# Row statistics of the closing stage scaled two pairs at a time on GpSimd, with norm, sum and store one turn later

## The chip, the core and the metric

The kernel runs on one core of a Trainium2 chip. A core has a matrix engine (TensorE, "PE" in the profile, with its weight loads as "PEld"), a vector engine (VectorE, "DVE"), an activation engine (ScalarE, "ACT"), a general engine (GpSimd, "POOL") and a small engine that here only starts transfers between the on-chip memory and DRAM (SyncE, "SP"; its list of issues is "SPq" in the profile). Each engine works through its own instructions in order and waits on semaphores for the others. The metric is the device time of one execution in microseconds; less is better.

## What is computed

The reference is a block of two residual layers on `x` of shape (8, 2048, 512), float32:

```python
x = x + _layernorm(_L0_attn_ref(_layernorm(x), ...))   # a long convolution from a state space model, then GELU
x = x + _layernorm(_L0_ffn_ref(_layernorm(x), ...))    # a gated recurrence over 8 steps and a last layer

def _layernorm(x, axis=-1, eps=1e-05):
    m = jnp.mean(x, axis=axis, keepdims=True)
    v = jnp.var(x, axis=axis, keepdims=True)
    return (x - m) / jnp.sqrt(v + eps)

# the end of _L0_ffn_ref
h = jnp.tanh(jnp.einsum('tbi,oi->tbo', x, wo) + c_final @ uo.T + bo)
```

The closing stage computes the last line of each: `h = tanh(z + u)`, with `z = x wo` already in DRAM and `u = c_final uo + bo`, then the layer norm of `h` over 512 values, and `x + norm(h)`, which is the output.

## The kernel before

The 2048 positions lie as 16 chunks of 128 partitions; 8 batch rows belong to each chunk. The recurrence runs over four quarters of four chunks each. The outputs of the first three quarters are made by `head` beside the matrix products of the next quarter. The last quarter has nothing after it: its outputs are made by `tail` (L1153), when the matrix products are over. This closing stage is what the change touches.

`tail` handles a pair of rows (two batch rows of one chunk, a 128x2x512 float32 block, 512 KB). The last quarter has 16 such pairs, numbered 0 to 15 here. For one pair there are these parts:

- `load` (L1162): SP loads the pair's `z` from DRAM. Each has a place of its own in the room of former weights.
- `load_x` (L1174): SP loads the pair's residual input `x` (`x1_d`; "x_d" in the profile). Nine places serve pairs 0 to 8. Pairs 9 to 14 use the places of pairs 0 to 5 again, so each of these six loads has to wait until the output of the pair nine places earlier has been stored from there. Pair 15 has a place of its own.
- `sum_` (L1179, L1180): twice an add of `u` on VectorE and a tanh on ScalarE.
- `stat` (L1183): `lnstat` (L462 to L465) on VectorE, two bn_stats, two bn_aggr and one small add of eps to the two variances; then `lnscale` (L471 to L476) on GpSimd, a power of -0.5, a product with the mean and a sign, on 128x2 values each.
- `norm` (L1187): ScalarE applies scale and bias to the two rows.
- `out` (L1192): the residual add of the two rows, on GpSimd; in every fourth pair the second row is added on VectorE.
- `store` (L1195): SP writes the pair to the output.

The order on each engine is written out by hand: the functions are called in the order in which the engines are to run them, inside `manual_schedule`, and this includes SP's issues. The loop at L1290 goes through turns n. In each it calls the parts by the list at L1293, whose second number is the delay: part `st_` is called for pair n - d. So turn n issues the load of `z` for pair n + 3, the load of `x` for pair n + 3, the store of pair n - 5, the sum of pair n - 1, the statistics of pair n - 2, and the norm and output add of pair n - 3. The first three pairs' loads and six further loads of `z` are issued earlier, so the loop issues `z` for pairs 9 to 15 and `x` for pairs 3 to 15. Every fourth turn also adds the bias to `u` of one chunk (L1098, VectorE).

Since SP's list is in order, a load that waits for a store to land holds back everything behind it in the list.

Of the kernel before, what the change touches and what calls it, by code (L numbers as in the profile page):

```python
# [11 lines left out]
F32 = mybir.dt.float32  # L12
I32 = mybir.dt.int32
AF = mybir.ActivationFunctionType
ALU = mybir.AluOpType
# [4 lines left out]
P = 128  # L20
# [9 lines left out]
EPS = 1e-5  # L30
# [29 lines left out]
def s4_gated_block(ctx, tc, a, dbg=None):  # L60
    nc = tc.nc
    V, S, T, Q = nc.vector, nc.scalar, nc.tensor, nc.gpsimd
# [41 lines left out]
    nhalf = const.tile([P, NB], F32, name="nhalf")  # L104
# [347 lines left out]
        T.matmul(out, lhsT=w(0), rhs=x(1), start=False, stop=stop)  # L452


    def lnstat(src, tag):

        n = len(src)
        st = FE.tile([P, n, 6], F32, name="st" + tag)
        mv = FE.tile([P, n, 2], F32, name="mv" + tag, bufs=2)
        rs = FE.tile([P, n], F32, name="rs" + tag, bufs=2)  # L460
        for i, v in enumerate(src):
            V.bn_stats(st[:, i], v)  # L462
        for i in range(n):
            V.bn_aggr(mv[:, i], st[:, i])
        V.tensor_scalar(rs, mv[:, :, 1], EPS, None, ALU.add)  # L465
        return n, mv, rs, tag

    def lnscale(s_, neg=True):

        n, mv, rs, tag = s_  # L470
        Q.tensor_tensor(rs, rs, nhalf[:, 0:n], ALU.pow)  # L471
        mu = mv[:, :, 0]
        if neg:
            mu = FE.tile([P, n], F32, name="nm" + tag, bufs=2)
            Q.tensor_tensor(mu, mv[:, :, 0], rs, ALU.mult)
            Q.tensor_scalar(mu, mu, -1.0, None, ALU.mult)  # L476
        return [(mu[:, i : i + 1], rs[:, i : i + 1]) for i in range(n)]
# [101 lines left out]
    with ExitStack() as cctx:  # L579
# [182 lines left out]
        for k in range(4):  # L762
            pmt = pm_.tile([P, 512], F32, name="pmt")
            lv, src = ((0, None), (0, 0), (1, 0), (1, 1))[k]
# [42 lines left out]
        for g in range(NG):  # L807
# [12 lines left out]
            if not nxt:  # L820
                ectx.close()
                FV = ctx.enter_context(tc.tile_pool(name="fv", bufs=1, side="right", reuse_waits="tile"))
                FE = ctx.enter_context(tc.tile_pool(name="fe", bufs=1, side="right", reuse_waits="tile"))
                fcol = FE.tile([P, 4, KT], F32, name="fcol")
            with tc.manual_schedule(engines=MAN if nxt else MAN | {mybir.EngineType.SP}):
# [17 lines left out]
                for s_ in range(NJ):  # L843
                    if s_ % 2 == 0 and s_:
                        conv_out(g, s_ // 2 - 1)
                    if nn:

                        d = ND1 if g == 1 else 0
# [125 lines left out]
    def part_a(key):  # L974

        q, t, kind, n = key
        z = kind == "z"
        u = units[key] = pu.tile([P, 4, BP], F32, name="u")
        for pr in FIRST:
            mms(u, places(key, pr), *views(key)[0], True, not t or z)  # L980
        if t and not z:
            mms(u, FIRST[0][:1] + FIRST[1] + FIRST[0][1:], *views(key)[1], False, True)
        if z:
            if n == 0:
                gates["z"] = FT.tile([P, 2, BP], F32, name="zc")
            c22 = gates["z"][:, n]
        else:
            g = gates[key] = FJ.tile([P, 4, BP], F32, name="gate2", tag="wq") if kind == 2 else FT.tile([P, 4, BP], F32, name=f"gate{kind}")
            c22 = g[:, 2]
        z_, v_ = (UV, UZ) if z else (UZ, UV)  # L990
        u2 = u2p[:, len(u2s) % 2]
        u2s.append(key)
        S.activation(u2, u[:, UX], AF.Copy)  # L993
        V.tensor_tensor(u2, u2, u[:, UY], ALU.add)  # L994
        V.tensor_tensor(c22, u2, u[:, z_], ALU.add)
        V.tensor_tensor(c22, c22, u[:, v_], ALU.add)
        V.tensor_tensor(u[:, 2:4], u[:, 2:4], u2[:, None].to_broadcast([P, 2, BP]), ALU.add)  # L997

    def part_b(key):

        q, t, kind, n = key
        u, z = units.pop(key), kind == "z"
        wx, wc = views(key)
        mms(u, places(key, THEN), *wx, False, z or not t)
        if z:
            zt, zc = FT.tile([P, 3, BP], F32, name="zt", bufs=2), gates["z"]
            S.activation(zt[:, 0], u[:, UX], AF.Copy)
            S.activation(zt[:, 1:3], u[:, 2:4], AF.Copy)

            def store():  # L1010
                o = z_d[QC * q + n, :, t], z_d[QC * q + n + 2, :, t]
                dma(out=o[0], in_=zt[:, 0:2].rearrange("p a b -> p (a b)"))
                dma(out=o[1][:, 0:BP], in_=zt[:, 2])
                dma(out=o[1][:, BP:], in_=zc[:, n])

            return store
        if t:
            mms(u, THEN, *wc, False, True)
        g = gates[key]
        bs = (bias if t else bias0)[:, kind]  # L1020
        act = lambda o, s_, b: S.activation(o, s_, AF.Tanh, scale=gsc[kind], bias=b)  # L1021
        act(g[:, 2], g[:, 2], bs[:, n + 2 : n + 3])
        act(g[:, 0:2], u[:, 0:3:2], bs[:, n : n + 1])
        act(g[:, 3], u[:, UZ], bs[:, n + 2 : n + 3])
        if kind == 2:
            V.scalar_tensor_tensor(g, gates.pop((q, t, 1, n)), 1.0, g, ALU.add, ALU.mult)  # L1026
        elif kind == 0:
            return state(q, t, n)
# [124 lines left out]
    def tail(q, cj, tp, n):  # L1153

        c, s_ = QC * q + cj, {}

        def load():
            w = (3, 1, 5, 2, 6, 0)[n // 3]
            if n % 3 == 0:
                tails[w] = (FW if w < 2 else FV if w == 2 else FT).tile([P, 3, 2, H], F32, name="zz", tag=f"w{w}", bufs=1)  # L1160
            s_["z"] = tails[w][:, n % 3]
            dma(out=s_["z"], in_=z_d[c, :, 2 * tp : 2 * tp + 2])  # L1162

        def load_x():
            i = (n + 3) % 9
            if n == 15:
                s_["x"] = tails[0][:, 1]
            elif i < 3:
                if i == 0:
                    tails[4] = FT.tile([P, 3, 2, H], F32, name="xw", tag="w4", bufs=1)  # L1170
                s_["x"] = tails[4][:, i]
            else:
                s_["x"] = (FJ, FJ, FE, FT, FJ, FT)[i - 3].tile([P, 2, H], F32, name="xx", tag=("wl", "ws", "y", "gate1", "wq", "gate0")[i - 3])
            dma(out=s_["x"], in_=x1_d[c, :, 2 * tp : 2 * tp + 2])  # L1174

        def sum_():
            for i in range(2):
                z = s_["z"][:, i]
                V.tensor_tensor(z, z, us_[c], ALU.add)  # L1179
                S.activation(z, z, AF.Tanh, scale=1.0 / SW)  # L1180

        def stat():
            s_["s"] = lnscale(lnstat([s_["z"][:, i] for i in range(2)], "h"))  # L1183

        def norm():
            for i, (nm, rs) in enumerate(s_["s"]):
                S.activation(s_["z"][:, i], s_["z"][:, i], AF.Identity, scale=rs, bias=nm)  # L1187

        def out():
            for i in range(2):  # L1190
                z, x = s_["z"][:, i], s_["x"][:, i]
                (V if n % 4 == 3 and i else Q).tensor_tensor(x, x, z, ALU.add)  # L1192

        def store():
            dma(out=a["out"][c, :, 2 * tp : 2 * tp + 2], in_=s_["x"])  # L1195

        return load, load_x, sum_, stat, norm, out, store

    tails = {}
    gsc = (0.5 / SW, 0.5 / SW, 1.0 / SW)  # L1200
    bias = FE.tile([P, 3, KT], F32, name="bias")
    bias0 = FE.tile([P, 3, KT], F32, name="bias0")
# [11 lines left out]
    def put(fs, base, ps):  # L1214
        for f, p in zip(fs, ps):
            todo.setdefault(base + p, []).append(f)

    def go(p):
        for f in todo.pop(p, ()):
            f()  # L1220
# [12 lines left out]
    rows = [tail(NQB - 1, cj, tp, 4 * cj + tp) for cj in range(QC) for tp in range(NB // 2)]  # L1233
# [4 lines left out]
    for n, (q, t) in enumerate(steps):  # L1238
        b = 16 * n
# [15 lines left out]
        if q and t:  # L1255
            for r in range(QC * NB):
                p = 3 * r + 17 - 16 * t
                if 0 <= p < 16:
                    put(head(q - 1, r // NB, r % NB), b, [p + d for d in (0, 2, 4, 6, 8, 9, 10, 12)])
    with tc.manual_schedule(engines=MAN | {mybir.EngineType.SP}):  # L1260
        before = None
        for n, (q, t) in enumerate(steps):
            zs = [(q, t, "z", i) for i in range(2)]
            gs = [(q, t, gt, mp) for mp in range(2) for gt in (1, 2, 0)]

            def finish(key, p):
                st_ = part_b(key)
                if st_:
                    put([st_], p, [1])

            for sl, key in enumerate(zs + gs if n else gs[:5] + zs + gs[5:]):
                p = 16 * n + 2 * sl
                part_a(key)
                go(p)

                late = n and t and sl == 2
                if sl == 3 and n and t:
                    finish(zs[1], p + 1)
                    before = gs[0]
                if before and not late:  # L1280
                    finish(before, p + 1)
                if not late:
                    before = key
                go(p + 1)
        part_b(before)
        for p in sorted(todo):
            go(p)
        for f in end[2:6]:
            f()
        for n in range(len(rows) + 5):  # L1290
            if n % 4 == 0 and n < len(rows):
                end[6 + n // 4]()
            for st_, d in ((0, -3), (1, -3), (6, 5), (2, 1), (3, 2), (4, 3), (5, 3)):  # L1293
                if 0 <= n - d < len(rows) and (st_ > 1 or n - d > (2 if st_ else 8)):
                    rows[n - d][st_]()

# [61 lines left out]
```

## Time and profile before

| what | value |
|---|---|
| median of 3 runs | 2808.93 us (2808.02 to 2810.8) |
| the profiled execution, its own time | 2808.14 us |
| its span, first to last instruction | 2806.4 us |
| busy over the span: PE, DVE, ACT, POOL | 2552.5, 2095.5, 1480.0, 1226.8 us |
| last matrix product of the last quarter's steps ends | about 2724 us |
| first sum of pair 0 on VectorE | 2737.68 us |
| sum of pair 15 on VectorE starts | 2789.56 us |
| last store issued, landed | 2802.80, 2805.4 us |

Times inside the execution count from the start of the span. The profiled execution's own time is 1.74 us more than its span. The matrix engine sets the time up to about 2737 us; the closing stage is the last 69 us, some 2.4% of the whole.

### The profile page before, as it was taken

The page shows a single profiled execution, that of the slowest core. Times are in us where ns is not written, and L with a number is a line of the kernel's source. Part 1 is how long each engine was busy: PE and PEld are TensorE (multiplying, and loading weights), DVE is VectorE, ACT ScalarE, POOL GpSimd, SP SyncE. Part 2 cuts the span into 40 slices and gives each one's busy share as a digit, 9 for nine tenths or more (in the row PEclk, how much of TensorE's full clock was granted, in tenths as well). Part 3 has the DMA queues.
Part 4 walks back from the last instruction along what each step waited for, and adds up shares of the span by engine and source line. Part 5 has one row for each costly group of instructions (what it writes and reads, how often), then busy time and mean ns, then how long its engine had stood idle before and what let it go on. Part 6 is the DMA issues. An engine that isn't in the chain of part 4 may idle for free.

```text
span 2806.4 us, 60001 instructions
## 1 busy us (share of the span) xinstructions
PE 2552.5 (91%) x23940; PEld 2229.7 (79%) x23940; DVE 2095.5 (75%) x4248; ACT 1480.0 (53%) x3091; POOL 1226.8 (44%) x1520
## 2 busy tenths in 40 slices
PE   4578888896999999999999999999999999999991
PEld 3367777785888888788898887888898788888870
DVE  7878888867667766677887777778777677777748
ACT  8966666654444444445555444455555454554436
POOL 5777777743112211124554431355554224543307
PEclk9799999998999999999999999999999999999995
DMA  6977887887334433225564432356554234543356
GB/s 236 304 238 241 259 257 246 257 282 209 99 86 126 106 98 91 80 91 150 164 180 138 142 102 95 109 162 178 155 165 129 91 106 136 166 121 102 104 170 234
DMA packets 507536, 449.25 MB, mean 160 GB/s; under 512 B 275574, under 2 KB 386680, under 8 KB 502264
## 3 DMA queue, kind: packets, MB, share of 16 engines
q1 hardware_dynamic: 506824, 444.90, 52.7%
q8 instruction: 187, 3.06, 0.4%
q14 instruction: 93, 0.76, 0.1%
q10 hardware_dynamic: 432, 0.52, 0.1%
HBM read 293.58 MB, written 151.78 MB: 159 GB/s over the span
## 4 chain that ended last, share of the span: by engine, by line
PE 62%; DVE 7%; ACT 3%; issue 1%; POOL 1%; DMA 0%; SPq 0%; POOLq 0%; DVEq 0%; ACTq 0%
PE u L955 60%; PE pt L485 2%; DVE zz L1179 1%; ACT gate L1021 1%; DVE u L997 1%; DVE cd L1042 1%; DVE gate L1041 0%; DVE cf L1056 0%; DVE sth L462 0%; ACT xf L101 0%; DVE u2p L994 0%; DVE xf L102 0%; PE u L451 0%; ACT zr L1145 0%; ACT cf L1054 0%
## 5 line engine op out<-in xcount | busy, mean ns | idle before, releaser
L955 PEld LDWEIGHTS <-w 128*128 128x128 f16 x15120 | 1481.0, 98 | 198.9 <-issue 16.0
L955 PE MATMUL u<-xf,w 128*128 128x256 f16 x8064 | 944.2, 273 | 17.8 <-DVE u L997 6.1
L955 PE MATMUL u<-cf,w 128*128 128x256 f16 x7056 | 825.7, 273 | 2.0 <-DVE cf L1056 2.0
L1021 ACT ACTIVATE gate<-u,bias 128x512 f32<-128x512 f32 (+1 forms) x384 | 200.9, 574 | 275.2 <-PE u L955 274.9
L993 ACT ACTIVATE u2p<-u 128x256 f32<-128x256 f32 x256 | 96.6, 379 | 436.9 <-PE u L955 436.8
L955 PE MATMUL u<-w,xf 128*128 128x256 f16 x2688 | 310.5, 273 | 4.0 <-DVE u L997 4.0
L1146 POOL TENSOR_TENSOR x1r<-x1r,zr 128x512 f32<-128x512 f32 x96 | 133.4, 1390 | 410.5 <-ACT zr L1145 295.2
L994 DVE TENSOR_TENSOR u2p<-u2p,u 128x256 f32<-128x256 f32 x256 | 106.7, 417 | 267.3 <-ACT u2p L993 265.9
L909 POOL TENSOR_TENSOR xr<-y,xr 128x512 f32<-128x512 f32 x120 | 160.7, 1360 | 300.0 <-ACT y L908 300.0
L955 PEld LDWEIGHTS <-xf 128*128 128x128 f16 x2688 | 263.0, 98 | 36.3 <-DVE u L997 5.5
L997 DVE TENSOR_TENSOR u<-u,u2p 128x512 f32<-128x512 f32 x256 | 179.0, 699 | 8.7
L646 POOL TENSOR_TENSOR u<-xg,u 128x512 f16<-128x512 f32 x104 | 129.2, 1242 | 106.7 <-ACT u L644 105.6
L471 POOL TENSOR_TENSOR rsy<-rsy,nhalf 128x2 f32<-128x2 f32 (+1 forms) x68 | 51.0, 751 | 281.6 <-DVE rsy L465 280.6
L640 POOL TENSOR_TENSOR xg<-xg,mu 128x512 f32<-128x512 f32 x112 | 162.8, 1460 | 6.0 <-DMA xg<-in_xr 6.0
L102 DVE TENSOR_TENSOR x<-pxt,x 128x256 f16<-128x256 f32 x240 | 100.1, 419 | 63.6 <-ACT x L101 62.3
L1026 DVE SCALAR_TENSOR_TENSOR gate<-gate,gate 128x1024 f32<-128x1024 f32 x64 | 90.0, 1406 | 69.6 <-ACT gate L1021 68.5
L1128 POOL TENSOR_TENSOR zr<-zr,ur 128x512 f32<-128x512 f32 x96 | 130.0, 1354 | 21.1 <-DMA zr<-z_d 12.3
L666 PE MATMUL pxt<-x,at 128*128 128x256 f16 x224 | 61.9, 277 | 79.3 <-DVE x L102 78.9
L462 DVE BATCH_NORM_STATS2 sty<-y 128x6 f32<-128x512 f32 x120 | 76.9, 682 | 76.1 <-DMA y<-y_d 76.1
L101 ACT ACTIVATE x<-pxt 128x256 f16<-128x256 f32 x240 | 91.5, 382 | 73.5 <-PE pxt L666 67.8
L451 PE MATMUL pyt<-u,t 128*128 128x128 f16 (+2 forms) x544 | 123.7, 227 | 0.0
L452 PE MATMUL pyt<-u,t 128*128 128x128 f16 (+2 forms) x544 | 123.3, 227 | 0.0
(373 smaller groups left out, 5261.1 us busy)
## 6 DMA issues: line engine op xcount, KB each, us to landing
xs<-in_rr SPq DMA_DIRECT2D x32, 1024.0 KB, 6.4
t<-kpad SPq DMA_DIRECT2D x32, 1024.0 KB, 5.6
y_d<-y SPq DMA_DIRECT2D x30, 1024.0 KB, 7.6
xr<-in_r SPq DMA_DIRECT2D x60, 512.0 KB, 5.8
xa<-x_d SPq DMA_DIRECT2D x120, 256.0 KB, 4.0
y<-y_d SPq DMA_DIRECT2D x59, 512.0 KB, 5.8
x_d<-xr SPq DMA_DIRECT2D x59, 512.0 KB, 3.1
xg<-in_xr SPq DMA_DIRECT2D x28, 1024.0 KB, 8.6
```

The lines of the kernel that those rows point to most:

```text
L102: V.tensor_tensor(lo, src, hi, ALU.subtract)
L451: T.matmul(out, lhsT=w(1), rhs=x(0), start=False, stop=False)
L452: T.matmul(out, lhsT=w(0), rhs=x(1), start=False, stop=stop)
L640: Q.tensor_tensor(xg, xg, bc(mu1), ALU.subtract)
L646: (V if g == 2 else Q).tensor_tensor(u[:, js, 1], xg, u[:, js, 0], ALU.subtract)
L909: Q.tensor_tensor(xv, yv, xv, ALU.add)
L955: T.matmul(u[:, d], lhsT=w(f, b, i == 1, k), rhs=x(f, b, i == 2, k), start=opens and bank not in seen, stop=stop and j == len(n) - 1, skip ...
L994: V.tensor_tensor(u2, u2, u[:, UY], ALU.add)
L997: V.tensor_tensor(u[:, 2:4], u[:, 2:4], u2[:, None].to_broadcast([P, 2, BP]), ALU.add)
L1021: act = lambda o, s_, b: S.activation(o, s_, AF.Tanh, scale=gsc[kind], bias=b)
L1128: Q.tensor_tensor(s_["z"], s_["z"], us_[c], ALU.add)
L1146: Q.tensor_tensor(s_["x"], s_["x"], s_["z"], ALU.add)
```

## The change

The statistics of a pair (`stat`) no longer include the eps add and the scale. They write mean and variance into one half of a buffer that two pairs share. A new part, `scale`, does something only for odd pairs: it takes the variances of two pairs together (128x2x2 values) and runs four GpSimd instructions, the eps add, the power, the product and the sign. The list of the turns becomes

```python
for n in range(len(rows) + 6):
    ...
    for st_, d in ((0, -3), (6, 6), (1, -3), (2, 1), (3, 2), (4, 4), (5, 4), (7, 2)):
```

so norm and output add are called for pair n - 4, the store for pair n - 6, and there is one turn more. On SP, a turn's order changes from z, x, store to z, store, x.

```diff
-    def lnstat(src, tag):
+    def lnstat(src, tag, eps=True):
...
-        V.tensor_scalar(rs, mv[:, :, 1], EPS, None, ALU.add)
+        if eps:
+            V.tensor_scalar(rs, mv[:, :, 1], EPS, None, ALU.add)
...
         def stat():
-            s_["s"] = lnscale(lnstat([s_["z"][:, i] for i in range(2)], "h"))
+            m = n % 2
+            if m == 0:
+                both[0] = [FE.tile([P, 2, *d], F32, name=nm, bufs=2) for nm, d in (("mvb", (2, 2)), ("rsb", (2,)))]
+                both[0] += [FE.tile([P, 2, 2], F32, name="nmb", bufs=2)]
+            mv, rs, nm = s_["b"] = both[0]
+            st = FE.tile([P, 2, 6], F32, name="stb", bufs=2)
+            for i in range(2):
+                V.bn_stats(st[:, i], s_["z"][:, i])
+            for i in range(2):
+                V.bn_aggr(mv[:, m, i], st[:, i])
+
+        def scale():
+            if n % 2:
+                mv, rs, nm = s_["b"]
+                Q.tensor_scalar(rs, mv[:, :, :, 1], EPS, None, ALU.add)
+                Q.tensor_tensor(rs, rs, nhalf[:, 0:4].rearrange("p (a b) -> p a b", a=2), ALU.pow)
+                Q.tensor_tensor(nm, mv[:, :, :, 0], rs, ALU.mult)
+                Q.tensor_scalar(nm, nm, -1.0, None, ALU.mult)
 
         def norm():
+            mv, rs, nm = s_["b"]
+            s_["s"] = [(nm[:, n % 2, i : i + 1], rs[:, n % 2, i : i + 1]) for i in range(2)]
             for i, (nm, rs) in enumerate(s_["s"]):
...
-        return load, load_x, sum_, stat, norm, out, store
-
-    tails = {}
+        return load, load_x, sum_, stat, norm, out, store, scale
+
+    tails, both = {}, {}
...
-        for n in range(len(rows) + 5):
+        for n in range(len(rows) + 6):
...
-            for st_, d in ((0, -3), (1, -3), (6, 5), (2, 1), (3, 2), (4, 3), (5, 3)):
+            for st_, d in ((0, -3), (6, 6), (1, -3), (2, 1), (3, 2), (4, 4), (5, 4), (7, 2)):
```

The other callers of `lnstat` keep the eps add on VectorE.

## The prediction

> **What bounds the kernel now.** I read three views in this order: the stage table (busy time by engine), the order of time on VectorE and GpSimd, and SP's waits with the landing times of single transfers. The change acts only after 2737 us, where the matrix engine has nearly finished. Columns of the first: stretch, its length, then busy time of PE, PEld, DVE, ACT, POOL, TensorE clock, DMA share, GB/s.
>
> ```profile
> 2737.68:2748.46 10.78, 7.00 (x33) 2.95 (x31) 10.57 (x25) 7.59 (x12) 4.76 (x8) 1.00 0.01 6
> 2748.46:2781.58 33.12, 0.00 (x0) 0.00 (x0) 32.27 (x68) 23.63 (x37) 29.78 (x43) 0.52 0.82 268
> 2781.58:2797.00 15.42, 0.00 (x0) 0.00 (x0) 14.27 (x28) 9.65 (x15) 13.87 (x20) 0.50 0.92 339
> 2797.00:2806.40 9.40, 0.00 (x0) 0.00 (x0) 1.41 (x1) 1.52 (x2) 5.60 (x7) 0.50 0.44 175
> ```
>
> VectorE is full (32.27 of 33.12), GpSimd nearly (29.78), and the transfers are busy 0.82 of the time: three near limits, not one. VectorE's fullness is partly a wait:
>
> ```profile
> 2749.57 1.27 DVE L462 BATCH_NORM_STATS2 sth<-zz 128x6 f32<-128x512 f32 x2
> 2750.77 0.29 DVE L464 BATCH_NORM_AGGREGATE mvh<-sth 128x2 f32<-128x6 f32 x2
> 2751.17 1.15 DVE L465 TENSOR_SCALAR rsh<-mvh 128x2 f32<-128x2 f32 x1
> ...
> 2749.80 2.49 POOL L1192 TENSOR_TENSOR xx<-xx,zz 128x512 f32<-128x512 f32 x2
> 2752.40 0.71 POOL L471 TENSOR_TENSOR rsh<-rsh,nhalf 128x2 f32<-128x2 f32 x1
> ```
>
> The eps add (128x2) takes 0.17 us when GpSimd is idle and 1.15 us when two output adds run there; it ends at 2752.32, with them (2752.29). The power can only start behind it. So the two engines go in lockstep, a pair in 3.8 us. Third, SP:
>
> ```profile
> SPq L1174 <- DMA out<-xx: 25.7, 6, 4.8
> ...
> 2781.58 0.32 SPq L1174 DMA_DIRECT2D xx<-x_d  x1
> 2782.00 0.38 SPq L1195 DMA_DIRECT2D out<-xw  x1
> 2782.42 0.43 SPq L1162 DMA_DIRECT2D zz<-z_d  x1
> ```
>
> Six loads of x (pairs 9 to 14) wait for a store of pairs 0 to 5 to land, 25.7 us in all. They are issued at 2751.88, 2758.00, 2763.90, 2769.66, 2775.53 and 2781.58: a chain with a mean hop of 5.94 us, slower than the lockstep. The last z, pair 15's, is issued only behind all of it, at 2782.42, and lands about 6.3 us later (the other z loads of this stretch: 6.1 to 6.4), at 2788.7. VectorE starts that pair's sum at 2789.56. The chain has 0.9 us to spare; it doesn't bind yet, but an earlier VectorE would meet it.
>
> **The change, part by part.** *Eps add off VectorE.* 16 instructions, mean 0.727 us, 11.6 us busy, leave; nearly all lies on VectorE's path (the last two not, there is no sum behind them). Without it a pair costs VectorE 1.19 (two sums) + 1.19 (two bn_stats) + 0.37 (bn_aggr with its gap) = 2.75 us, plus three bias adds and three output adds of 0.7 and about 0.65 us wait for the norm before each of these. Alone it could start sum 15 about 8 us earlier.
>
> *GpSimd.* Per pair it now pays 0.72 + 0.20 + 0.22 with gaps = 1.26 us. After, per two pairs: eps add 0.25 (the L609 row, a like add there), power on 128x4, 0.20, 0.22 and gaps. The power on 4 values isn't in the trace; 128x2 takes 0.72, 128x8 takes 1.67, these bound it, and the line between gives 1.03. Sum 2.0 us per two pairs in place of 2.5 plus the waits for the eps add. With seven output adds of 1.25 per four pairs it needs 12.8 us where it takes 15.05 today (the power of pair 6 to that of pair 10, 2763.57 to 2778.62, shows the period).
>
> The Trainium skill, "GPSIMD Engine Reference", section "Engine selection", speaks against this part: it puts elementwise adds on VectorE, GpSimd being about twice as slow with two inputs. By it eight adds of twice 0.17 us would cost 2.7 us; by the row above they cost 2.0, and either is less than the 11.6 us that go.
>
> *One turn later.* The first store: bn_aggr of pair 1 ends at 2744.3, GpSimd's scale at 2746.4. ScalarE's order puts tanh 3 ahead of norm 0, and VectorE does the bias add (0.7) and sum 3 first, so norm 0 starts at 2747.0, the two output adds at 2747.75, and store 0 goes at 2750.3 instead of 2748.46.
>
> *SP's order.* z, x, store becomes z, store, x with the store one turn later, and x of pair n+9 still needs store n landed. The hops stay six in number. But seen from an issued x, the queue was x, store, z and becomes x, z, store: the store that the next x waits for moves from second to third place. Landings after their own issues, in order of issue (x at 2758.00, store at 2758.41, z at 2758.84):
>
> ```profile
> xx<-x_d SPq DMA_DIRECT2D x1, 512.0 KB, 4.6
> ...
> out<-xx SPq DMA_DIRECT2D x1, 512.0 KB, 5.5
> zz<-z_d SPq DMA_DIRECT2D x1, 512.0 KB, 6.3
> ```
>
> From the x issue that is 4.6, 5.9 and 7.1 us: the three end in turn, 1.25 apart. So the hop has 5.94 us as its lower bound (place is immaterial) and 5.94 + 1.25 = 7.19 as its upper. A burst of x loads before the stage (issued at 2730.91, 2731.33, 2731.76, the third landing 5.7 after its issue) gives 6.55 for third place. In the turns measured, the last z is still arriving for 1.1 us when the next x is issued, which will no longer be; so slightly less than 7.15. I take **7.0**, nearer the rows of this same trio.
>
> The skill's "DMA: Bandwidth & Descriptors", section "Anatomy of one DMA — SWDGE (gpsimd) path", has about 2.0 us fixed plus bytes/436e9 for one transfer. For 1.5 MB on end that estimates 5.6 us a hop, and would bring z 15 early enough for a gain; but it estimates 4.4 us for the two transfers of today's hop, where the trace has 5.94, so the rows decide.
>
> *The sum.* Store 0 at 2750.3 has the queue to itself (z 9 now goes ahead of it, long before). The last store lands 2.6 us after issue, store 0 with z behind it took 3.4; I take 2.7: x 9 at 2753.0. Five hops of 7.0: x 14 at 2788.0. z 15 follows, second in line, landing about 5.7 after x (second place: 5.9 in that stretch, 4.9 in the burst): 2793.7. Sum 15 starts at 2793.8, not 2789.56. Before that VectorE has run ahead and stands idle for z 13, 14 and 15. From s = sum 15's start: tanh ends at s+1.95 (as today); norm 12 stands behind it on ScalarE, so the first output add of pair 12 starts at s+2.65; pairs 12 and 13 take 5.0 on GpSimd, s+7.65; then scale for 14 and 15, behind them in GpSimd's list, s+9.7; half a norm 0.8; pair 14's adds 2.5, s+13.0; pair 15's last add 1.71 (today's row), store issue, 2.6 to landing and 1.0 to the end as today: s+18.4. Today it is 16.84 (2789.56 to 2806.4). End of span 2812.2, +5.8 us: 4.2 from the late z, 1.6 from the longer tail. With the 1.74 us around the span **2814.0 us**. That is 5.9 above this execution's own 2808.14, and 5.1 (0.18%) above the median shown.
>
> VectorE's 11.6 us therefore turn into a wait for z. Each 0.1 us on the hop is 0.5 us at the end; each 0.1 us on the wide power only 0.1.
>
> **Rivals.** *A, place in line is immaterial* (SP's issue gap and the fixed latency make the hop, 5.94): x 14 at 2782.7, z 15 lands 2788.4, end 2806.9, time 2808.6: no difference. For it: a hop holds about 2 us in which hardly any data moves (DMA share 0.82). Against: the three landings lie one transfer time apart.
>
> *B, the chain doesn't bind* (the store lands much faster when no z trails it): then GpSimd sets the end. From 2747.75: 21 output adds of 1.25 and six scales of 1.95 = 37.9, pair 12 at 2785.7; + 5.0 + 1.95 + 0.85 + 2.5 + 1.75 + 3.6 = 2801.4, time 2803.1, faster by 5.8 us or 0.21%. It needs z 15 landed by 2783, a hop under 4.9 us; decisive point 5.9. For it: a lone store takes 2.6. Against: x and z both stand in front of it.
>
> *C, a worse hop.* Writes behind two reads slow further, as the backlogged stores of today's end (8.1 to 9.7 us to landing) do behind their likes. At 7.6 the end comes 3.0 us later, time 2817.0. Against: here nothing else is queued.
>
> *D, scaling by twos costs more than it saves on GpSimd* (power at the 128x8 price): 0.6 us in the tail, inside the range.
>
> **How the numbers follow.** About 0.2%, some 5.6 us, is what a measurement of this kernel can tell from no change. Forecast (hop 6.6 to 7.3, so 2812.0 to 2815.5) 0.68, which lies across the bound at 2814.5; since the next run's level may differ by 1 us, I split it 0.40 slower, 0.28 within. A 0.12, within. B 0.09, faster. C 0.11, slower. So faster 0.09, same 0.40, slower 0.51. The range: down to A's 2808.6 and up to C's 2817.0.
>
> **What would show it.** Right: SP's wait of L1174 for stores grows from 25.7 to about 33 us; the x issues from pair 9 on are 6.6 to 7.3 apart; VectorE's L1179 waits some 10 us in all for loads of zz; L465 is gone after 2737; GpSimd's power runs 8 times at 128x4, about 1.0 us; sum 15 starts near 2794, the first store at about 2750. Wrong: if hops stay at 5.9 or fall, or VectorE never waits for zz, the step that failed is the place in line; if the tail from sum 15 isn't near 18.4 us, it is the order of pairs 12 to 15 on ScalarE and GpSimd.

## The result

The changed kernel takes 2816.46 us (median of 9, 2814.82 to 2817.87); the kernel before took 2808.02 us (median of 9) in the same runs. The ratio is 1.0029, with a 95% interval of 1.0019 to 1.0039: slower by about 8 us. The time lies inside the range of 2808.6 to 2817.0, 2.5 us over the forecast of 2814.0 and 1.0 us over the band of 2812.0 to 2815.5 that the prediction held for likeliest.

The profiled execution took 2815.61 us, its span is 2813.8 us. The closing stage starts at a slightly different moment in each execution (its first bias add on VectorE began between 2733.65 and 2738.94 us in the profiles below), and the moments of the two kernels and their variants overlap. So the stage is compared from the start of the first bias add to the end of the span: 2806.4 - 2736.95 = 69.45 us before, 2813.8 - 2736.24 = 77.56 us after, 8.1 us more, where the medians differ by 8.4.

**The profile after.** The stage table of the changed kernel, with the columns as before (stretch, length, busy PE, PEld, DVE, ACT, POOL, clock, DMA share, GB/s):

```profile
2764.00:2772.00 8.00, 0.00 (x0) 0.00 (x0) 6.06 (x16) 5.24 (x10) 6.66 (x9) 0.50 0.66 201
2772.00:2780.00 8.00, 0.00 (x0) 0.00 (x0) 6.47 (x12) 5.45 (x10) 6.09 (x8) 0.50 0.71 231
2780.00:2788.00 8.00, 0.00 (x0) 0.00 (x0) 3.27 (x9) 3.98 (x6) 6.67 (x9) 0.50 0.68 228
2788.00:2796.00 8.00, 0.00 (x0) 0.00 (x0) 4.41 (x8) 2.64 (x4) 3.81 (x6) 0.50 0.70 222
2796.00:2804.00 8.00, 0.00 (x0) 0.00 (x0) 3.52 (x10) 4.05 (x6) 5.66 (x6) 0.50 1.03 420
```

No engine is full any more, and the transfers, at 0.66 to 0.71, move less than in the kernel before (0.82) until 2796. Everything waits for something. What for, by the waits and VectorE's order of time:

```profile
SPq L1175 <- DMA out<-xx: 32.9, 6, 6.6
...
DVE zz L1180 <- DMA zz<-z_d: 7.6, 3, 4.6
...
2788.16 1.28 DVE L1180 TENSOR_TENSOR zz<-zz,u 128x512 f32<-128x512 f32 x2 [4.59 <-DMA zz<-z_d]
2795.44 1.29 DVE L1180 TENSOR_TENSOR zz<-zz,u 128x512 f32<-128x512 f32 x2 [2.74 <-DMA zz<-z_d]
```

SP waits 32.9 us for stores (25.7 before), and VectorE stands idle for z 13 (0.3 us), 14 and 15. Sum 15 starts at 2795.44. The loads of x from pair 9 on go out at 2752.04, 2759.50, 2767.42, 2774.78, 2782.06 and 2789.40: a mean hop of 7.47 us instead of 5.94. Landing times after their own issues, for the three transfers at 2767.42, 2767.79 and 2768.32:

```profile
xx<-x_d SPq DMA_DIRECT2D x1, 512.0 KB, 4.0
...
zz<-z_d SPq DMA_DIRECT2D x1, 512.0 KB, 5.7
...
out<-xx SPq DMA_DIRECT2D x1, 512.0 KB, 6.4
```

From the issue of x that is 4.0, 6.1 and 7.3 us. With the old order it was 4.6 (x), 5.9 (store) and 7.1 (z): the store is last instead of second, and the second of two reads in a row lands 2.0 us after the first (1.8 to 2.0 in the other hops), not 1.25.

There is a second wait which the prediction doesn't have. GpSimd in the changed kernel, bracket: idle before and what ended it:

```profile
2762.35 5.08 POOL L1212 TENSOR_TENSOR xx<-xx,zz 128x512 f32<-128x512 f32 x4 [1.44 <-ACT zz L1207]
2767.51 0.23 POOL L1198 TENSOR_SCALAR rsb<-mvb 128x4 f32<-128x4 f32 x1
2767.82 1.04 POOL L1199 TENSOR_TENSOR rsb<-rsb,nhalf 128x4 f32<-128x4 f32 x1
2768.94 0.20 POOL L1200 TENSOR_TENSOR nmb<-mvb,rsb 128x4 f32<-128x4 f32 x1
2769.23 0.23 POOL L1201 TENSOR_SCALAR nmb<-nmb 128x4 f32<-128x4 f32 x1
2770.39 3.71 POOL L1212 TENSOR_TENSOR xw<-xw,zz 128x512 f32<-128x512 f32 x3 [0.93 <-ACT zz L1207]
```

The scale of pairs 6 and 7 (2767.51) is listed behind the output adds of 4 and 5, though its input was ready at 2764.9. Only behind it can ScalarE make norm 6, and only behind that GpSimd has its next add: 0.93 us idle here, 1.44 us there. Four pairs take 15.5 us (adds of pairs 0 and 4 start at 2746.80 and 2762.35), not the 12.8 of the prediction and even more than the 15.05 before. While the chain of stores holds z back, this shows only in part (experiment 9).

### The profile page after: what moved, and what is told of

Same layout as the page of the kernel before. It is cut to its first block, busy times and chain, and to the rows that moved or that the text cites. A ratio compares the mean times of both kernels' runs of the same rounds, so it can differ in the third digit from the quotient of the medians.

```text
span 2813.8 us, 59941 instructions
## 1 busy us (share of the span) xinstructions
PE 2549.9 (91%) x23940; PEld 2228.0 (79%) x23940; DVE 2087.2 (74%) x4232; ACT 1479.6 (53%) x3091; POOL 1223.0 (43%) x1504
## 4 chain that ended last, share of the span: by engine, by line
PE 62%; DVE 6%; ACT 3%; POOL 1%; issue 1%; DMA 1%; SPq 0%; POOLq 0%; ACTq 0%; DVEq 0%
PE u L956 59%; PE pt L486 2%; ACT gate L1022 1%; DVE u L998 1%; DVE cd L1043 1%; DVE gate L1042 0%; ACT xf L101 0%; DVE cf L1057 0%; DVE zz L1180 0%; DVE xf L102 0%; DVE u2p L995 0%; ACT cf L1055 0%; PE u L451 0%; PE u L450 0%; DVE sty L462 0%
```

## The experiments

All start from the changed kernel or the kernel before and alter a few lines of the closing stage. The table has, for each profiled execution, the time from the first bias add to the start of sum 15, from there to the end of the span, the sum of the two, and the measured ratio to the kernel before.

| kernel | to sum 15 | tail | stage, us | ratio, 95% interval |
|---|---|---|---|---|
| before | 52.61 | 16.84 | 69.45 | 1 |
| changed | 59.20 | 18.36 | 77.56 | 1.0029, 1.0019 to 1.0039 |
| 1 changed, SP's old order | 54.03 | 18.43 | 72.46 | 1.0011, 1.0002 to 1.0020 |
| 2 before, SP's new order | 56.31 | 15.75 | 72.06 | 1.0009, 1.0001 to 1.0018 |
| 3 changed, z ahead | 54.01 | 18.49 | 72.50 | 1.0014, 1.0005 to 1.0023 |
| 4 changed, z ahead, scale first | 47.22 | 17.83 | 65.05 | 0.9986, 0.9977 to 0.9994 |
| 5 before, z ahead | 52.56 | 16.79 | 69.35 | 0.9995, 0.9986 to 1.0004 |
| 6 changed, SP's old order, scale first | 54.18 | 17.42 | 71.60 | 1.0008, 0.9999 to 1.0017 |
| 7 as 4, eps add on VectorE | 47.06 | 18.11 | 65.17 | 0.9983, 0.9974 to 0.9992 |
| 8 as 4, more adds on VectorE | 48.62 | 17.29 | 65.91 | 0.9987, 0.9979 to 0.9996 |
| 9 changed, scale first | 57.50 | 17.47 | 74.97 | 1.0024, 1.0014 to 1.0034 |
| 10 before, eps add on GpSimd | 54.14 | 17.84 | 71.98 | 1.0011, 1.0002 to 1.0021 |

A stage 2.8 us longer is 0.1% of the time, so the differences of the stage and the ratios can be set against each other; they agree to about 1.3 us.

**1. The changed kernel with SP's old order.**

```diff
-            for st_, d in ((0, -3), (6, 6), (1, -3), (2, 1), (3, 2), (4, 4), (5, 4), (7, 2)):
+            for st_, d in ((0, -3), (1, -3), (6, 5), (2, 1), (3, 2), (4, 4), (5, 4), (7, 2)):
```

> The changed kernel with only SP's part undone: the turn's list has z, x, store of pair n - 5 again; statistics, scale, norm and output add stay as changed. Theory 1 (place in line: behind z the store lands later, and the hop sets the end): hops from the load of x for pair 9 on fall from 7.5 to 5.9 us, z of pair 15 lands near 2789, sum 15 starts there, the tail of 18.4 us stays, end of span near 2807, 6.6 us under the changed kernel. Theory 2 (besides, norm now waits behind the wide scale, which stands behind two output adds on GpSimd, and four pairs take 15.5 us there instead of 15.05): the end comes near 2809, 4.7 us under the changed kernel, and GpSimd's adds of pair 12 start near 2793.4 as its own period sets them, not sum 15. Rival (place immaterial): hops stay at 7.4 and the time with them.

The loads of x went out at 2755.42, 2761.26, 2767.07, 2772.98, 2778.85 and 2784.79: hops of 5.87 us. Landings for the three transfers at 2767.07, 2767.50 and 2767.91:

```profile
xx<-x_d SPq DMA_DIRECT2D x1, 512.0 KB, 4.7
...
out<-xx SPq DMA_DIRECT2D x1, 512.0 KB, 5.5
...
zz<-z_d SPq DMA_DIRECT2D x1, 512.0 KB, 6.3
```

The store is second again and lands 5.9 us after x. The stage lost 5.1 of the 8.1 us, less than the 6.6 that the chain alone would give and near the 4.7 of theory 2: VectorE's sums now wait for z 0.2 us in all, and sum 15 comes behind the output add of pair 11 on VectorE, which waits 3.16 us for its norm:

```profile
2791.89 1.16 DVE L1212 TENSOR_TENSOR xx<-xx,zz 128x512 f32<-128x512 f32 x1 [3.16 <-ACT zz L1207]
```

That the place in line is immaterial is refuted.

**2. The kernel before with SP's new order.**

```diff
-        for n in range(len(rows) + 5):
+        for n in range(len(rows) + 6):
...
-            for st_, d in ((0, -3), (1, -3), (6, 5), (2, 1), (3, 2), (4, 3), (5, 3)):
+            for st_, d in ((0, -3), (6, 6), (1, -3), (2, 1), (3, 2), (4, 3), (5, 3)):
```

> The kernel before with only SP's part of the change: z, store, x with the store of pair n - 6; all else as before. Theory 1: hops of 7.4 us, the last x of the chain at 2788, z of pair 15 lands at 2794, sum 15 then, tail 16.8 as before: span 2811, 4.8 us over the kernel before. Rival (the loss comes from the compute part, one turn later and GpSimd's work): within 1 us of the kernel before.

Hops of 7.21 us (x at 2751.33 to 2787.38), and sum 15 waits for z:

```profile
2793.45 1.29 DVE L1179 TENSOR_TENSOR zz<-zz,u 128x512 f32<-128x512 f32 x2 [3.65 <-DMA zz<-z_d]
```

Sum 15 came 3.7 us later than in the kernel before (4.4 expected); the stage grew by 2.6 us only, not by 4.8, since the tail is 1.1 us shorter: while z 15 is awaited, GpSimd works off what it has, and then waits 2.81 us for VectorE. The order of SP's three issues is harmful by itself.

**3 and 4. z ahead of the chain, and then the wide scale first.** The loads of z for pairs 9 to 15 have places of their own and need not stand in the chain (z 15 still goes out in the first hop, behind x 9). The first added line is experiment 3, the second experiment 4.

```diff
-            for st_, d in ((0, -3), (6, 6), (1, -3), (2, 1), (3, 2), (4, 4), (5, 4), (7, 2)):
+            for st_, d in ((6, 6), (1, -3), (0, -9), (2, 1), (3, 2), (4, 4), (5, 4), (7, 2)):
+            for st_, d in ((6, 6), (1, -3), (0, -9), (2, 1), (3, 2), (7, 2), (4, 4), (5, 4)):
```

> The changed kernel with the loads of z for pairs 9 to 15 issued in turns 0 to 6, ahead of the chain of stores, so that no sum waits for it. If the chain were the only cause, the end would come as the prediction's rival B has it, span near 2801, 12 us under the changed kernel and some 5 under the kernel before. Theory 2 (GpSimd's own loop takes over): output adds of pairs 0, 4, 8 and 12 lie 15.5 us apart as in the changed kernel, pair 12 at 2793.4, end near 2809: 4.7 us under the changed kernel, still 2.7 over the kernel before.

> As the last, and in each turn the wide scale is called ahead of norm and output add, so on GpSimd it stands ahead of the pair n - 4's adds and the next norm need not wait for it. Theory 2: the idle time on GpSimd before output adds (2.4 us in four pairs) goes, four pairs take about 12.8 us there, the adds of pair 12 start near 2785, and with scale, and adds of 12 to 15 in a row the end comes near 2800 to 2801, 13 us under the changed kernel and 6 under the kernel before. If theory 2 is wrong it ends where the last one ends.

With z ahead alone the stage takes 72.50 us, the same as in experiment 1, which reached it by another way: it is GpSimd's loop that stands there, and the prediction's rival B, 2801 for the end of the span, is refuted too. The output adds of pairs 0, 4 and 8 start at 2747.36, 2762.92 and 2778.59, 15.6 us apart. With the scale ahead of the adds the loop opens:

```profile
2764.64 0.23 POOL L1198 TENSOR_SCALAR rsb<-mvb 128x4 f32<-128x4 f32 x1
2764.95 1.04 POOL L1199 TENSOR_TENSOR rsb<-rsb,nhalf 128x4 f32<-128x4 f32 x1
2766.07 0.20 POOL L1200 TENSOR_TENSOR nmb<-mvb,rsb 128x4 f32<-128x4 f32 x1
2766.36 0.23 POOL L1201 TENSOR_SCALAR nmb<-nmb 128x4 f32<-128x4 f32 x1
2766.56 2.50 POOL L1212 TENSOR_TENSOR xx<-xx,zz 128x512 f32<-128x512 f32 x2
2769.01 2.48 POOL L1212 TENSOR_TENSOR xw<-xw,zz 128x512 f32<-128x512 f32 x2
```

The add starts 0.2 us after the scale's last instruction does, instead of 1.16. Four pairs take 13.35 us (2748.71, 2762.01, 2775.42), the stage 65.05: 7.4 us less than without the reordering and 4.4 less than the kernel before, where 6 were expected (12.8 us for four pairs). The chain is still there (x and store alone, hops of 5.8 us from pair 10 to pair 14), but nothing that the engines need early stands in it.

**5. The kernel before with z ahead.**

```diff
-            for st_, d in ((0, -3), (1, -3), (6, 5), (2, 1), (3, 2), (4, 3), (5, 3)):
+            for st_, d in ((1, -3), (6, 5), (0, -9), (2, 1), (3, 2), (4, 3), (5, 3)):
```

> The kernel before with its loads of z for pairs 9 to 15 ahead of the chain of stores (turns 0 to 6), nothing else changed. All theories: z of pair 15 had 0.9 us to spare there, so the stage (first bias add to the end of the span, 69.45 us in the kernel before, 77.56 in the changed one) stays within 1 us of 69.45 and the time within 0.1%. If it got faster by more, z would have bound the kernel before as well, and the gain of the run with z ahead and scale first would not come from the wide scale.

69.35 against 69.45 us: as expected. The kernel before was not bound by z, and the gain of experiment 4 comes from the compute part: scaling by twos, with the wide scale first and norm and output add a turn later. These weren't taken apart.

**6 and 9. Scale first, with z left in the chain**, with SP's old order (6, the first line) and its new one (9, the second).

```diff
+            for st_, d in ((0, -3), (1, -3), (6, 5), (2, 1), (3, 2), (7, 2), (4, 4), (5, 4)):
+            for st_, d in ((0, -3), (6, 6), (1, -3), (2, 1), (3, 2), (7, 2), (4, 4), (5, 4)):
```

> The changed kernel with SP's old order and the wide scale called ahead of norm and output add; z stays in the chain. Theory: hops of 5.9 us, the chain's last x 45.9 us after the first bias add and z of pair 15 landed 7.1 later, at 53; VectorE could start sum 15 at 47.2 as with z ahead, so it waits for z some 5 us; with a tail of 17.8 the stage takes 70.8 us: 5.8 over the run with z ahead and scale first (65.05) and 1.3 over the kernel before. If the chain with its old hop doesn't matter, the stage takes 65 us.

> The changed kernel with the wide scale called ahead of norm and output add; SP's order stays as changed, z stays in the chain. If the lengthened chain alone decides there, the stage from the first bias add to the end stays at 77 (77.56 in the changed kernel, less the half microsecond by which the tail of the run with scale first is shorter), and the order on GpSimd, worth 7.4 us with z ahead, brings less than 1 us here. If the order on GpSimd is the cause by itself, the stage falls by several us, towards 70.

Experiment 6 takes 71.60 us (70.8 expected; one of its hops was 7.1 us): VectorE waits 7.6 us for z in all, and the 6.6 us over experiment 4 are the price of z in the chain even with the old hop. Experiment 9 missed its mark: 74.97 instead of 77. VectorE waits 10.9 us for z, so the chain decides, but the reordering still brought 2.6 us, not less than 1. 1.7 of them are an earlier sum 15 (57.50 instead of 59.20), and 1.2 of these are the first hop: 6.26 us instead of 7.46, with store 1 issued 1.5 us behind z, since its adds were later, instead of 0.5 (the last section comes back to this). The rest is the shorter tail, 17.47 us.

**7. Experiment 4 with the eps add back on VectorE.**

```diff
-                Q.tensor_scalar(rs, mv[:, :, :, 1], EPS, None, ALU.add)
+                V.tensor_scalar(rs, mv[:, :, :, 1], EPS, None, ALU.add)
```

> As z ahead and scale first, with the eps add of two pairs (128x4) back on VectorE, 8 instructions in place of 16. If what the change gains is to keep the eps add from waiting for GpSimd's output adds, each of the 8 waits up to 1.1 us on VectorE and GpSimd's power stands behind it: GpSimd saves 0.31 us a scale and loses as much or more in waits, stage 65 to 67 us. If the eps add's engine is immaterial and only the pairing and the order count, the stage gets shorter by about 2 us (GpSimd's 8 adds gone).

65.17 us, 0.1 us from experiment 4. That is at the edge of the first expectation, but the waits on VectorE that it rests on hardly occur (median of the 8 adds 0.19 us, one of 1.16). The 2 us of the second don't come either: GpSimd stands idle for 0.33 us before three of the powers, and three others, which start during VectorE's output adds, take 1.49 instead of 1.04 us. On which engine the eps add runs is immaterial here.

**8. Experiment 4 with the second add of every odd pair on VectorE.**

```diff
-                (V if n % 4 == 3 and i else Q).tensor_tensor(x, x, z, ALU.add)
+                (V if n % 2 and i else Q).tensor_tensor(x, x, z, ALU.add)
```

> As z ahead and scale first, with the second output add of every odd pair on VectorE (8 of 32, so far 4). GpSimd has no idle time left there, so if it sets the stage, four adds of 1.25 us less there bring 3 to 4 us, less what the adds on VectorE wait for GpSimd's own (1.4 us each in place of 0.7): stage 61 to 63 us. If VectorE or the stores set the end, nothing is gained.

65.91 us: no gain, expectation missed. GpSimd now waits 0.7 to 1.5 us for a norm before the adds of every second pair, because VectorE itself waits 0.69 us for the norm before each add, and with it the next sums. Four pairs take 13.8 us. In experiment 4 both engines were close to their limits already, each busy 12.4 of the 13.35 us.

**10. The kernel before with the eps add of each pair on GpSimd, and nothing else.**

```diff
+            st4 = lnstat([s_["z"][:, i] for i in range(2)], "h", eps=False)
+            Q.tensor_scalar(st4[2], st4[1][:, :, 1], EPS, None, ALU.add)
+            s_["s"] = lnscale(st4)
```

`lnstat` has the argument `eps` here as in the change.

> The kernel before with the eps add of each pair on GpSimd (128x2) and nothing else: no pairing, no later turn, no change on SP. VectorE is freed of waits that cost it about 0.7 us a pair, GpSimd has 16 adds of 0.24 us and their gaps more, 1.3 us in four pairs, against 0.6 us of waits and 0.4 us of stretched powers saved. If GpSimd sets the stage, it takes 15.1 to 15.4 us for four pairs instead of 15.05 and the stage 69.5 to 71 us (69.45 before): the move alone brings nothing. If VectorE's wait was the cost, four pairs take about 13 us and the stage 62 us or what the last z allows.

71.98 us, 2.5 more than before and 1 over the expectation; four pairs take 15.70 us on GpSimd, which now waits for nobody from its first output add on. VectorE runs ahead and then waits 3.1 to 3.3 us for the norm before each of its output adds. GpSimd's waits in the kernel before, and one of VectorE's here:

```profile
POOL rsh L471 <- DVE rsh L465: 53.8, 5, 50.6
...
2787.53 1.41 DVE L1195 TENSOR_TENSOR xx<-xx,zz 128x512 f32<-128x512 f32 x1 [3.19 <-ACT zz L1190]
```

Of the first line's 53.8 us, all but 1.7 lie ahead of GpSimd's first output add. So GpSimd set the kernel before, and VectorE's fullness was the waiting of an engine that had nothing to gain.

## Why the prediction was right, and where it wasn't

**SP's order, right in mechanism, too small in size.** The store moved behind z, the hops grew, z 15 came late and VectorE waited for it: experiments 1 and 2 show it from both sides. The mis-sized term is the hop: it was taken as 7.0 us and measured 7.47 (7.21 in experiment 2), above the band of 6.6 to 7.3. The bound "5.94 + 1.25 = 7.19" came near the store's landing of 7.3, but in part by luck: 1.25 us is the spacing of a read, a write and a read, while here x lands some 0.5 us sooner and z 1.8 to 2.0 us behind it. What failed is the step down from the bound to 7.0. It was argued from the z of the hop before, which would no longer be arriving beside the next x; but hops with nothing behind the store (experiment 4, 5.8 us) are less than 0.1 us shorter than those with a z behind it (experiment 1, 5.87). That step is 1.0 us in five hops. The first two hops, 7.46 and 7.92 us, make another 1.0 over the bound, the last three 0.4; why single hops are longer stays open, and the old order has some too (7.14 in experiment 6, 6.88 and 6.95 in experiment 10). In all, five times 0.47 us are 2.35 us. Sum 15 started 6.04 instead of 5.8 us behind the last x of the chain, which is 0.24 more, and x 9 went out 15.80 instead of 16.05 us after the first bias add, which gives as much back. So sum 15 came 2.35 us later than predicted, and that is all of what the stage misses: 77.56 against 2812.2 - 2736.95 = 75.25.

**First store, tail, wide power: right.** The first store, from issue to the x behind it, took 2.71 us (2.7), the tail 18.36 (18.4), the power on 128x4 1.04 (1.03). The eps add on GpSimd took 0.23 to 0.24 us (0.25) five times, but 0.55 the three times that it started during an output add of VectorE: 2.8 us for the eight, not 2.0. The 2.7 us that the prediction sets beside the 2.0 is nearer by luck: it doubles 0.17 us by a factor for two inputs, and the eps add has one.

**VectorE's 11.6 us, right that nothing comes of them, for a reason only half seen.** The prediction lets them end in a wait for z of some 10 us. That wait came to 7.6 us; besides, VectorE's three output adds ahead of sum 15 waited 3.44, 3.44 and 0.69 us for the norm, where the prediction has 0.65 each. But without the chain there would have been no gain either (72.50 us in experiment 3): VectorE was full because it stood in step with GpSimd, and experiment 10 shows that freeing it by giving GpSimd the adds costs 2.5 us. The 8 us by which sum 15 could start earlier were too many: with the chain and the order put right it is 5.4 (experiment 4).

**GpSimd's 12.8 us for four pairs: wrong.** That sum adds up busy times and leaves out the list's order: the wide scale behind two pairs' adds, the next norm behind the scale, the next adds behind the norm, 2.4 us idle in four pairs. Measured are 15.5 us, and 13.35 once the scale stands first. The late z hid this error, which was luck: by GpSimd's loop alone sum 15 starts 54.01 us after the first bias add (experiment 3), and the predicted chain put it at 56.85; a chain 3 us shorter would have laid the error bare. Rival B, built on the same sum, would have been wrong by 8 us on the stage (experiment 3: 72.50; B: 64.5).

**Rivals.** A, place immaterial: refuted by experiment 1. B: the hop, 7.47 us, is far over its 5.9, and its end of 2801 fell with experiment 3. C, a hop of 7.6: its size is nearest to what came, as one hop of 7.92 and one of 7.46 were there, but no other stores were queued in them; the mean of the other three was 7.33. D: not seen.

In sum, of the 8.1 us, 5.1 come with SP's order (experiment 1 takes them away) and 3.0 with the order on GpSimd and the later turn, which remain whether z comes sooner by the old order or ahead of the chain (72.46 and 72.50). Together they cost more than each alone added up (2.6 in experiment 2, 3.0 in 1 and 3). Scaling by twos pays only with z out of the chain and the scale first: 4.4 us on the stage, a ratio of 0.9986 (experiment 4). SP's old order with the scale first isn't enough (experiment 6).

## What to carry to other kernels

Read an in-order list as a chain before adding up its busy times: ask of each moved instruction what stands ahead of it, and who waits for the one behind. On a transfer queue with a load that waits for a store, the hop is the store's landing, so put nothing between them and take everything with a free place out of the chain. And an engine that is full may be waiting inside its instructions: here the eps add took 1.15 us beside two of GpSimd's output adds and 0.17 without, and only GpSimd's time counted.

## What wasn't expected of the hardware

Two loads of 512 KB in a row with a store close behind landed 1.8 to 2.0 us apart (x 4.04, z 6.06 us after the first issue), a load and a store behind it 1.2 to 1.3 us apart (4.7 and 5.9; 4.6 and 5.8 in experiment 4). A load followed by another load landed itself sooner, mostly at 4.0 to 4.2 us instead of 4.5 to 4.8. Why wasn't tried. And a hop of x and store with no z behind them (experiment 4, 5.8 us) is as long as one with a z behind (5.87): what stands behind the store is free.

A store that was issued later even landed earlier. The first hop has the same three transfers, x 9, z 15 and store 1, in experiments 3, 4, 7 and 8. Where the store was issued 0.5 us behind z, the hop took 7.18 us (3) and 7.30 (8), and z landed 5.6 and 5.7 us after its issue. Where the store was issued 1.4 to 1.6 us behind z, the hop took 6.24 us (7) and 6.53 (4), and z landed after 4.6 and 4.9 us. That the store close behind the two loads is the cause wasn't tried.
